# A graph layer in one program: the opening reordered, and the sums of the edge features spread one at a step

## The chip, the cores and the metric

The program runs on one core of a Trainium2 chip. Five engines work side by side, each through its own list of instructions: TensorE (PE: matrix products, with its weight loads, PEld, as a lane of their own in the profile), VectorE (DVE), ScalarE (ACT), GpSimd (POOL) and SyncE (SP). SP issues the ordinary transfers, POOL the indirect ones, which fetch rows by a list of row numbers. The metric is device microseconds of one execution.

## The reference

The layer has 6250 nodes, 206250 edges and 64 features, all in 32-bit floats. The edges are given in the order of their destination `dst`; every node has one edge to itself, and the others are random.

```python
h   = maximum(layernorm(x), 0)                   # 6250 x 64
msg = h[src] + edge_attr                         # 206250 x 64
agg = segment_sum(msg, dst, 6250)                # 6250 x 64
out = x + relu(agg @ W1 + b1) @ W2 + b2          # W1 64 x 128, W2 128 x 64
```

So two sums are wanted for each node: that of `h[src]` over its edges, and that of the edge features over its edges. Which edges belong to a node is known only when the program runs.

## The kernel before

**Sum of h[src] by counts.** For most of the edges the kernel gathers nothing. For each tile of three nodes it counts how often each source occurs among the tile's edges, and multiplies the counts with h, which stays in SBUF as `h2`, 49 blocks of 128 rows. A tile holds up to 127 edges. Three nodes with more edges than that are an "overfull triple"; there is room for 14 of them (`NX`), and each gets a second tile, which starts at its 128th edge.

84 tiles are a **block** of 252 nodes; 23 blocks cover the nodes that are counted. A block is worked in 14 **steps** of 6 tiles. The program is one list of 318 steps written by hand, and all engines get their instructions in that order; so a step number below is a place in the list, not a time. What a step does, in order: first the functions listed for it in the dictionary `before` (and those of `tops`). Then, on odd steps, `count` (line 936): 12 matmuls of a tile each (L943) into one of two PSUM buffers `pc`, and ACT's copy of the counts into `ring` (L952). On every third step DVE makes the rows for 18 more tiles (`rows_of_tiles`, two instructions of L930), on every sixth it encodes the keys of 36 tiles (L913, L919). Then, at the steps 1, 3, 5 and 7 of a block, come 12 or 13 of the 49 `products` of the block before (L962: counts by h, into the PSUM tile `pv`); at step 8 DVE adds `pv` to the sums (L997). So each block has a *product half*, steps 1 to 7, and a *sum half* behind it. Then the MLP of a finished block, where its steps begin (`LAYERS`: at step 11 or 5; the hidden layer L1040, two steps later its product L1048, then an addition and a store). Then what is listed in `later` and `turns` for the step, then the check whether a group of gathered edges may be summed, and last the gathers, as many as are due.

**Sum of the edge features.** 42 nodes in a row are a **chunk**; its edges lie within 1536 rows that follow one another, which SP loads as one tile `feat` (384 KB, six buffers). Of chunks there are six in a block, taken in three pairs. For a pair DVE makes a selector (`chunk_hot`, L487: which edge belongs to which node), at the steps `HOT_AT`; for each chunk PE does 24 pairs of a weight load and a matmul (`chunk_sum`, L498) into a PSUM tile `bank`, at the steps `CHUNKS`, and behind them the load of the chunk three pairs on is issued. At a step of the next block DVE copies the six sums out of PSUM (`take_sums`, L506, at `TAKE`), and PE adds them to that block's `pv` (`chunk_place`, L528, at `PLACE`).

**The gathered edges.** The last 20 groups of 1024 edges are done the other way: POOL gathers their rows of h from a table in DRAM and adds them to the edge features in SBUF (L348, `pfeat`, eight gathers of 128 rows for a group, three buffers). Such a group is summed by 8 matmuls of 128 rows (L559) two steps after its check. The check stands at the steps `GROUPS` of a block. It goes by a clock that the program keeps as it is written (`HEAD_US` 1.7 us for a step of the first block, `STEP_US` 1.04 for each later one, `GATHER_US` 2.0 for a gather): a group is taken at the first such step for which the clock of two steps on is four microseconds past its last gather. Taking a group frees its buffer, and the gathers of the group three further on are queued. POOL has other indirect DMAs in the same queue: the rows of edge data for a set of tiles (`words`, 15 in all), the lists of destinations (`dst`).

**The opening.** Before the steps begin, the layernorm is computed in three parts (`norm_mean` to `norm_h`), the positions of the edges are sought (`fetch_row`, `seek`, `place`), the first two tiles of the chunks' starts are worked out (`chunk_starts`, `chunk_rows`, `chunk_quarters`, `chunk_columns` with its index copy L421, `chunk_index`), and h is written to the table. In the first 14 steps, the first block, there are no products; at the steps `SECOND` seven functions find the overfull triples: ends, flags, ranks, picks, words (60 matmuls of one row or 14, 30 of them in L849), found (L855), fetch. `split_upper` and `split_lower` (L623) turn h into the two forms that the products need; they stand at the steps 10, 15 and 17 and one behind each. `clear` empties the sums at five steps from 18 on.

Of the kernel before, what the change touches and what calls it, by code (L numbers as in the profile page):

```python
# [10 lines left out]
F32 = mybir.dt.float32  # L11
# [11 lines left out]
P = 128  # L23
# [58 lines left out]
SECOND = (9, 10, 11, 12, 13, 14, 15)  # L82
FIRST = 12
PART = (0, 0, 12, 12, 24, 24, 36, 36, HI)
CHUNKS = ((9, 9), (11, 11), (13, 13))
FEATS = 6
FIRST_CHUNKS = ((9, 9), (11, 11), (13, 13))
LAST_CHUNKS = ((5, 5), (9, 9))
HOT_AT = (3, 6, 10)
TAKE = (4, 0)  # L90
PLACE = (6, 3)

GROUPS = (1, 3)
LAST_GROUPS = (1, 5)
LAYERS = {11: 2, 5: 2}
# [54 lines left out]
def gnn_kernel(ctx: ExitStack, tc: tile.TileContext, x, src_t, dst_t, dst_g, edge, w1, b1, w2, b2, out):  # L150
# [677 lines left out]
    def second_picks():  # L828
        flag, ends, prk = flags["flag"], flags["ends"], flags.pop("rank")
        fl = small.tile([P, 4, IC], F32, name="fl")  # L830
        rank, one = fl[:, 0, :], fl[:, 1, :]
        of = fl[:, 2:4, :].rearrange("p a i -> p i a")
        nc.vector.tensor_scalar(of[:, :, 0], nfirst, float(V), None, op0=OP.add)
        nc.vector.tensor_scalar(of[:, :, 1], ends[:, :IC], float(SLOTS), float(EA), op0=OP.add, op1=OP.min)
        nc.vector.tensor_scalar(one, nfirst, float(DUMP), None, op0=OP.subtract)
# [4 lines left out]
        flags["pick"], flags["of"], flags["one"] = pick, of, one  # L840

    def second_words():
        pick, of, one = flags["pick"], flags["of"], flags["one"]
        pxn = ps.tile([P, 2 + NX], F32, tag="po", name="pxn", bufs=1)
        px, pn = pxn[:, :2], pxn[:, 2:]
        for i in range(IC):
            nc.tensor.matmul(px[:NX, :], pick[:, i, :], of[:, i, :], start=(i == 0), stop=(i == IC - 1))
        for i in range(IC):
            nc.tensor.matmul(pn[:1, :], one[:, i:i + 1], pick[:, i, :], start=(i == 0), stop=(i == IC - 1))  # L849
        flags["found"] = px, pn  # L850

    def second_found():
        px, pn = flags.pop("found")
# [3 lines left out]
        nc.vector.tensor_scalar(second_n, pn[:1, :], float(DUMP), float(DUMP), op0=OP.add, op1=OP.min)  # L857
        flags["i"] = second_i
# [64 lines left out]
    def rows_of_tiles(j):  # L923
        if j * HT >= TILES:
            return
# [208 lines left out]
    chunk_quarters(0, 2)  # L1134
    chunk_columns(0, 2, "pc", 2)
# [11 lines left out]
    for g in range(GA + 2, GA + ROWS):  # L1147
# [7 lines left out]
        6: [lambda: chunk_turn(0)],  # L1155
        8: [lambda: place(7, 8)],
# [4 lines left out]
        93: [lambda: chunk_columns(2, NT)],  # L1161
        95: [lambda: chunk_index(2, NT)],
# [12 lines left out]
    for n, f in zip(SECOND, (second_ends, second_flags, second_ranks, second_picks, second_words, second_found, second_fetch)):  # L1175
# [58 lines left out]
    later = {}  # L1234

# [7 lines left out]
    for b in range(NW):  # L1243
        n = b * STEPS
        for u, at_c, at_h in zip(of_block[b], FIRST_CHUNKS if b == 0 else CHUNKS if b < NW - 1 else LAST_CHUNKS, HOT_AT):
            at_step(n + (at_c[0] - 2 if b == 0 else at_h), chunk_hot, u)
            for c in range(units[u][2]):
                at_step(n + at_c[c], chunk_sum, u, c)
        if b < NW - 1:
            at_step(n + STEPS + TAKE[b > 0], take_sums, b)  # L1250
# [206 lines left out]
```

## Time and profile before

| | |
|---|---|
| median of 3 runs | 430.98 us (428.21 to 432.04) |
| the profiled execution | 428.6 us, with a span of 426.6 us |
| instructions in it | 17243 |
| granted clock of PE, mean | 0.978 of full speed |
| busy: PE / PEld | 354.8 / 316.7 us |
| busy: ACT / DVE / POOL | 329.1 / 313.8 / 311.2 us |
| gathers of the groups (L348, pfeat) | 156 of 1693 ns |
| chunk sums (L498) | 3240 pairs |
| counts (L943) | 1904 matmuls |
| products (L962) | 1127 matmuls of 288 ns |

The span is the time from the first instruction to the last in the profiled execution; the time of the same execution is 2.0 us longer. A row of groups reads: line, engine, operation, what is written from what, number, then busy time, mean time of one in ns, and the idle time of the engine ahead of them with what ended most of it. A row of the timeline reads: start, duration, engine, line, operation, tiles and shapes, how many instructions, and in brackets the idle time just before and its end. A busy engine is not one at its peak, since matmuls are pipelined and their ends are modelled.

### The profile page before, as it was taken

Reading aid. Unit: us, or ns where it says so; the run is one execution under the profiler, and the core shown is the slowest. Engines: PE = TensorE matmul, PEld = TensorE weight load, DVE = VectorE, ACT = ScalarE, POOL = GpSimd, SP = SyncE. Lnnn points to the kernel's source line nnn. Section 1 sums busy time; section 2 is a strip of 40 time slices with the busy share of each in tenths; the row PEclk is TensorE's granted clock in tenths of the full one; section 3 lists DMA queues with packets and bytes.
Section 4 is the critical chain, followed back from the end, with each engine's and each line's share of the span. In section 5 each row is a group of like instructions: output and inputs, shape, how many; then the busy total and the mean of one; then the engine's idle time right before and its main releaser. Section 6 shows DMA issues by size and latency. Waiting matters only on the chain.

```text
span 426.6 us, 17243 instructions
## 1 busy us (share of the span) xinstructions
PE 354.8 (83%) x7299; PEld 316.7 (74%) x7300; DVE 313.8 (74%) x813; ACT 329.1 (77%) x378; POOL 311.2 (73%) x230
## 2 busy tenths in 40 slices
PE   2032399989988989969899799999999899999993
PEld 1022378879977878849799698788889789888893
DVE  6677879988996769728698378967697668868531
ACT  5475569898998678957899679887888789888630
POOL 8575588888888888888870868888888748888600
PEclk9999999999999999988999799999999999999997
DMA  7836994969795766939578569669759757977500
GB/s 166 245 112 198 342 225 90 253 144 242 195 241 134 191 155 155 283 48 269 126 177 252 158 136 265 168 160 242 188 133 273 197 156 200 250 179 173 138 15 18
DMA packets 114817, 77.73 MB, mean 182 GB/s; under 512 B 34356, under 2 KB 110252, under 8 KB 114734
## 3 DMA queue, kind: packets, MB, share of 16 engines
q1 hardware_dynamic: 88480, 66.72, 51.6%
q0 software_dynamic: 24016, 9.06, 16.9%
q8 instruction: 59, 0.97, 0.9%
q10 hardware_dynamic: 2238, 0.79, 0.8%
q14 instruction: 24, 0.20, 0.1%
HBM read 72.29 MB, written 4.26 MB: 179 GB/s over the span
## 4 chain that ended last, share of the span: by engine, by line
PE 66%; DVE 10%; ACT 8%; issue 6%; DVEq 0%; ACTq 0%
PE pv L962 25%; PE bank L498 15%; PE pc L943 11%; ACT ring L952 6%; PE ph L1040 3%; PE po L1048 3%; DVE hotb L930 2%; PE bank L559 2%; PE pv L528 2%; PE pk L749 1%; DVE hotf L487 1%; DVE at L913 1%; PE pw L756 1%; DVE xl L607 1%; PE pcols L416 1%
## 5 line engine op out<-in xcount | busy, mean ns | idle before, releaser
L348 POOL DMA_INDIRECT pfeat<-table,src_p x156 | 264.1, 1693 | 72.7 <-issue 42.4
L952 ACT ACTIVATE ring<-pc 128x1764 fp32r<-128x1764 uint8 (+3 forms) x181 | 260.3, 1468 | 45.1 <-PE pc L943 31.5
L962 PE MATMUL pv<-ring,h 128*128 128x252 f32 (+1 forms) x1127 | 156.2, 288 | 0.1
L962 PEld LDWEIGHTS pv<-ring,h 128*128 128x128 f32 x1127 | 138.9, 190 | 0.6 <-issue 0.3
L930 DVE TENSOR_TENSOR hotb<-at,of 127x576 int32<-127x576 bf16 x212 | 118.3, 601 | 1.9 <-DVE of L919 0.5
L498 PE MATMUL bank<-feat,hotf 128*18 128x64 f32 x3240 | 80.3, 229 | 17.1 <-issue 15.9
L943 PE MATMUL pc<-hotb 128*128 128x49 fp8e5 x1904 | 80.7, 187 | 9.5 <-DVE hotb L930 5.9
L943 PEld LDWEIGHTS <-hotb 128*128 128x128 fp8e5 x1904 | 69.2, 99 | 20.3 <-issue 6.1
L498 PEld LDWEIGHTS bank<-feat,hotf 128*18 128x18 f32 x3240 | 57.4, 101 | 30.0 <-issue 26.3
L487 DVE TENSOR_TENSOR hotf<-rel,iota 128x432 f32<-128x432 bf16 x68 | 40.7, 599 | 12.6 <-PE pc L943 10.0
L997 DVE TENSOR_TENSOR sums<-sums,pv 128x252 f32<-128x252 f32 (+3 forms) x28 | 8.4, 327 | 27.7 <-PE pv L962 20.8
L506 DVE COPY after<-bank 128x384 f32<-128x384 f32 (+2 forms) x23 | 12.6, 547 | 21.6 <-PE bank L498 19.2
L913 DVE TENSOR_TENSOR at<-iota_a,kq 128x576 bf16<-128x576 bf16 (+1 forms) x53 | 23.9, 451 | 0.3
L348 POOL DMA_INDIRECT words<-packed,first_i x15 | 17.1, 1140 | 7.4 <-issue 4.0
L1042 ACT ACTIVATE after<-ph,b1s 128x252 f32<-128x252 f32 (+3 forms) x26 | 12.0, 460 | 12.6 <-PE ph L1040 11.7
L348 POOL DMA_INDIRECT sums<-in_dst_g,row_i x15 | 16.7, 1116 | 4.6 <-issue 4.0
L769 ACT ACTIVATE kq<-pk 128x512 bf16<-128x512 f32 (+17 forms) x48 | 17.7, 442 | 3.0 <-PE pc L943 1.0
L1040 PE MATMUL ph<-sums,w1s 128*128 128x252 f32 (+3 forms) x52 | 18.0, 430 | 1.7 <-DVE sums L1009 1.3
L300 PE MATMUL psrc<-shift,src 128*64 128x128 f32 (+1 forms) x16 | 3.9, 419 | 18.2 <-ACT src L297 18.2
L919 DVE TENSOR_TENSOR of<-of,kv 128x288 bf16<-128x288 bf16 (+1 forms) x53 | 16.5, 312 | 2.9 <-ACT sums L366 0.5
L1048 PE MATMUL po<-w2s,after 128*126 128x64 f32 (+3 forms) x104 | 16.9, 287 | 0.8 <-ACT after L1042 0.6
L300 PEld LDWEIGHTS psrc<-shift,src 128*64 128x64 f32 (+1 forms) x16 | 2.8, 188 | 18.2 <-ACT src L297 13.5
(186 smaller groups left out, 318.4 us busy)
## 6 DMA issues: line engine op xcount, KB each, us to landing
feat<-in_edge SPq DMA_DIRECT2D x135, 384.0 KB
pfeat<-in_edge SPq DMA_DIRECT2D x19, 256.0 KB
pfeat<-table,src_p POOLq DMA_INDIRECT x156
out_y<-after SPq DMA_DIRECT2D x23, 63.0 KB
xl<-in_x SPq DMA_DIRECT2D x2, 512.0 KB
table<-xl SPq DMA_DIRECT2D x2, 512.0 KB
after<-in_x SPq DMA_DIRECT2D x4, 252.0 KB
table<-xl SPq DMA_DIRECT2D x1, 544.0 KB
```

What stands on the lines that cost most here:

```text
L348: nc.gpsimd.indirect_dma_start(out=rows, out_offset=None, in_=source, in_offset=bass.IndirectOffsetOnAxis(ap=index, axis=0), compute_op=op)
L487: nc.vector.tensor_tensor(hot_of[u][:, :n].rearrange("p c j w -> p (c j) w"), rel[:, c:c + n].rearrange("p c q k -> p (c q k)").unsqueeze( ...
L498: nc.tensor.matmul(bank[q * QP:q * QP + WQ, at:at + D], hot_of[u][:, c, j, :], feats[u][c][:, j, :], start=(k == 0), stop=(k == JP - 1))
L769: nc.scalar.activation(kq[:, q, at:at + n].rearrange("s i k o -> s (i k) o"), pk[:, q, a:a + n].rearrange("s i k -> s (i k)").unsqueeze(2) ...
L913: nc.vector.tensor_tensor(to[:, :n].rearrange("s i k (m o) -> s (i k) m o", o=2), iota_k.rearrange("s (m o) -> s m o", o=2).unsqueeze(1).t ...
L919: nc.vector.tensor_tensor(pairs_of, pairs_of, kv[:, c:c + n].rearrange("s i k o -> s (i k) o").unsqueeze(2) .to_broadcast([P, 2 * n, WE // ...
L930: nc.vector.tensor_tensor(hot[:SLOTS, :n, c:c + m * A8].rearrange("s i (w a) -> s i w a", a=A8), at[:SLOTS, o:o + n, k].unsqueeze(2).to_br ...
L943: nc.tensor.matmul(pc[:, j * WPC:j * WPC + HI], hot[:, :P], hot[:, P:P + HI], start=True, stop=True)
L952: nc.scalar.activation(to[:, h:z], of[:, h:z, u:v, :V], AF.Copy)
L962: nc.tensor.matmul(pvs[b], h2[:, h, :], ring[:, h, c:c + columns_of_block(b)], start=(h == 0), stop=(h == HI - 1))
L1040: nc.tensor.matmul(ph[:, :n], w1s, agg[:, start[b]:start[b + 1]], start=True, stop=True)
L1048: nc.tensor.matmul(po[:pairs[b], k, :], hid[:, k:2 * pairs[b]:2], w2s, start=True, stop=True)
```

## The change

*Opening.* The second set of rows (`rows_of_tiles(1)`) is made between `chunk_quarters` and `chunk_columns`, ahead of the end of the norm; in its old place, step 0, it is left out. `place(7, 8)` moves from step 8 to 6. The search for the overfull triples has nine functions at the steps 7, 8, 9, 10, 11, 13, 14, 20 and 22 in place of seven at 9 to 15: the node number of a triple becomes a third column of the matmuls that find its tile, so that 30 matmuls of `second_words` go, and is turned into a row later, by one matmul at step 20 (`second_turn`) and a DVE instruction at 22. The third chunk pair of the first block moves from step 13 to 15, which is the second step of block 1 and there stands behind the products; its selector moves to step 13.

*Steady blocks.* Block 1 keeps two chunks at each of the steps 9, 11 and 13. In the blocks 2 to 21 the six chunks stand at 7 and 9, 9 and 11, 13 and 15 (the last is step 1 of the next block). Those at 7 and 15 are put ahead of the products of their step (the new dictionary `soon`); of the two at 9 the one that comes first in its pair goes into `turns`, behind the other. `take_sums` and `chunk_place` go from steps 0 and 3 of the next block to 2 and 5 for these blocks, since the sixth sum now ends at step 1. The second pair's selector is made at step 5 in place of 6.

*Groups and MLP.* The checks for a group stand at the steps 1 and 7 of a block in place of 1 and 3, the second MLP at 7 in place of 5. Two steps in the work on later chunk starts come one and two steps sooner.

```diff
-SECOND = (9, 10, 11, 12, 13, 14, 15)
+SECOND = (7, 8, 9, 10, 11, 13, 14, 20, 22)
...
-CHUNKS = ((9, 9), (11, 11), (13, 13))
+EARLY_CHUNKS = ((9, 9), (11, 11), (13, 13))
+CHUNKS = ((7, 9), (9, 11), (13, 15))
 FEATS = 6
-FIRST_CHUNKS = ((9, 9), (11, 11), (13, 13))
+FIRST_CHUNKS = ((9, 9), (11, 11), (15, 15))
 LAST_CHUNKS = ((5, 5), (9, 9))
-HOT_AT = (3, 6, 10)
-TAKE = (4, 0)
-PLACE = (6, 3)
-
-GROUPS = (1, 3)
+HOT_AT = (3, 5, 10)
+TAKE = (4, 0, 2)
+PLACE = (6, 3, 5)
+
+GROUPS = (1, 7)
 LAST_GROUPS = (1, 5)
-LAYERS = {11: 2, 5: 2}
+LAYERS = {11: 2, 7: 2}
...
     def second_words():
...
         for i in range(IC):
             nc.tensor.matmul(px[:NX, :], pick[:, i, :], of[:, i, :], start=(i == 0), stop=(i == IC - 1))
-        for i in range(IC):
-            nc.tensor.matmul(pn[:1, :], one[:, i:i + 1], pick[:, i, :], start=(i == 0), stop=(i == IC - 1))
-        flags["found"] = px, pn
+        flags["found"] = px
...
+    def second_turn():
+        pn = ps.tile([P, NX], F32, tag="po", name="psecond", bufs=1)
+        nc.tensor.matmul(pn[:1, :], flags.pop("nodes"), ident[:NX, :NX], start=True, stop=True)
+        flags["turned"] = pn
+
+    def second_nodes():
+        nc.vector.tensor_scalar(second_n, flags.pop("turned")[:1, :], float(DUMP), float(DUMP), op0=OP.add, op1=OP.min)
...
     def rows_of_tiles(j):
-        if j * HT >= TILES:
+        if j * HT >= TILES or j in hots:
             return
...
     chunk_quarters(0, 2)
+    rows_of_tiles(1)
     chunk_columns(0, 2, "pc", 2)
...
         5: [lambda: chunk_nodes(0)],
-        6: [lambda: chunk_turn(0)],
-        8: [lambda: place(7, 8)],
+        6: [lambda: chunk_turn(0), lambda: place(7, 8)],
...
-        93: [lambda: chunk_columns(2, NT)],
-        95: [lambda: chunk_index(2, NT)],
+        92: [lambda: chunk_columns(2, NT)],
+        93: [lambda: chunk_index(2, NT)],
...
             at_step(n + (at_c[0] - 2 if b == 0 else at_h), chunk_hot, u)
             for c in range(units[u][2]):
-                at_step(n + at_c[c], chunk_sum, u, c)
+                k = at_c[c]
+                when = later
+                if 1 < b < NW - 1:
+                    when = soon if k in (7, STEPS + 1) else turns if (k, c) == (9, 0) else later
+                when.setdefault(n + k, []).append(lambda u=u, c=c: chunk_sum(u, c))
         if b < NW - 1:
-            at_step(n + STEPS + TAKE[b > 0], take_sums, b)
+            at_step(n + STEPS + TAKE[min(b, 2)], take_sums, b)
             for u in of_block[b]:
-                at_step(n + STEPS + PLACE[b > 0], chunk_place, u)
+                at_step(n + STEPS + PLACE[min(b, 2)], chunk_place, u)
...
             encode(n // (EB // ST) + 1)
+        for f in soon.pop(n, []):
+            f()
         if b and 1 <= s < FRESH:
             products(b - 1, PART[s], PART[s + 1])
```

25 lines of the change are left out of this document (13 added, 12 removed).

## The prediction

> **What bounds the kernel now.** I read the page first, for the chain and the groups.
>
> ```profile
> span 426.6 us, 17243 instructions
> ...
> PE 66%; DVE 10%; ACT 8%; issue 6%; DVEq 0%; ACTq 0%
> ...
> L348 POOL DMA_INDIRECT pfeat<-table,src_p x156 | 264.1, 1693 | 72.7 <-issue 42.4
> L952 ACT ACTIVATE ring<-pc 128x1764 fp32r<-128x1764 uint8 (+3 forms) x181 | 260.3, 1468 | 45.1 <-PE pc L943 31.5
> ```
>
> TensorE (PE) holds 66% of the chain that ended last, but ScalarE (ACT) copies counts for 260.3 us and GpSimd (POOL) gathers for 264.1 us, so each half of a block has to be looked at by itself. The busy times by window give this (length, then busy time of PE, its weight loads (PEld), VectorE (DVE), ACT and POOL, the granted clock, DMA). The first is block 1, the second all of the blocks 2 to 21, the next three are single blocks (from one start of products to the next), the last two the product half and the sum half of an ordinary one.
>
> ```profile
> 63.66:78.74 15.08, 13.88 (x298) 12.53 (x295) 13.87 (x37) 14.21 (x12) 12.89 (x8) 1.00 0.54 120
> 78.74:397.01 318.27, 295.23 (x6294) 264.34 (x6289) 244.68 (x630) 267.32 (x289) 250.01 (x155) 0.98 0.75 192
> 139.33:158.63 19.30, 17.44 (x352) 15.34 (x349) 13.14 (x39) 12.39 (x12) 16.25 (x11) 1.00 0.65 159
> 174.43:196.87 22.44, 18.77 (x331) 15.79 (x327) 11.59 (x28) 15.30 (x18) 18.70 (x13) 0.85 0.62 153
> 227.12:246.22 19.10, 16.96 (x321) 14.63 (x317) 10.87 (x27) 14.15 (x16) 9.25 (x7) 0.84 0.65 186
> 353.33:361.70 8.37, 8.37 (x128) 8.07 (x124) 7.91 (x27) 7.95 (x12) 7.15 (x5) 1.00 0.82 205
> 361.70:367.83 6.13, 5.90 (x203) 4.96 (x200) 4.89 (x12) 5.44 (x6) 5.21 (x4) 1.00 0.76 203
> ```
>
> The 20 steady blocks take 318.27 us. Without the three long ones (60.84) the other 17 take 15.14 each: a product half of 8.4, in which PE is busy throughout, and so 6.7 for the sum half. In the sum half quoted PE has holes (4.96 of 6.13 loading weights) and ACT needs 5.44: ACT is the floor there, 0.7 below. The waits of the steady stretch say what the holes are.
>
> ```profile
> PEld bank L498 <- issue: 24.4, 52, 0.6
> ACT ring L952 <- PE pc L943: 19.7, 39, 2.5
> POOL pfeat L348 <- DMA pfeat<-in_edge: 19.5, 2, 13.0
> ```
>
> Fifty-two times PE stops in the middle of a feature sum with no semaphore to wait for, 24.4 us or 1.2 per block. The timeline shows when.
>
> ```profile
> 316.27 0.47 PE L943 MATMUL pc<-hotb 128*128 128x49 fp8e5 x12
> ...
> 316.68 0.84 PE L498 MATMUL bank<-feat,hotf 128*18 128x64 f32 x37
> 316.71 1.69 POOL L348 DMA_INDIRECT pfeat<-table,src_p  x1 [0.30 <-issue]
> ...
> 317.97 0.23 PEld L498 LDWEIGHTS bank<-feat,hotf 128*18 128x18 f32 x10 [0.61 <-issue]
> ```
>
> A gather starts at 316.71, PE issues 37 pairs of the sum, stops, and goes on 1.26 us after the start of the gather. I read it so: for about 1.2 us of each gather PE gets no new instructions and lives on those it holds, some 32 to 37 pairs. Products, 49 of them in the 8.37 us of a half, never use these up; a run of 48 sums does in 0.8 us.
>
> Two blocks hit this hard: two short gathers in a row leave PE starved.
>
> ```profile
> 237.00 0.99 POOL L348 DMA_INDIRECT words<-packed,first_i  x1 [0.30 <-issue]
> ...
> 238.29 1.42 POOL L348 DMA_INDIRECT words<-packed,first_i  x1 [0.30 <-issue]
> 238.31 0.15 PEld L498 LDWEIGHTS bank<-feat,hotf 128*18 128x18 f32 x4 [0.59 <-issue]
> ...
> 239.06 0.15 PEld L498 LDWEIGHTS bank<-feat,hotf 128*18 128x18 f32 x4 [0.59 <-issue]
> ```
>
> Four pairs run per 0.75 us, and the clock granted in these two blocks is 0.85 and 0.84. Over 15.14 they cost 7.30 and 3.96, of which the clock is 0.15 x 22.44 = 3.4 and 0.16 x 19.10 = 3.1.
>
> **The change, part by part.** The sum starts from the profiled execution, 428.6 us with a span of 426.6; the median of the runs is 430.98, 2.4 above it.
>
> *The head.* Rows of its timeline:
>
> ```profile
> 38.16 0.16 DVE L421 CAST cols_i<-pcols 128x2 int32<-128x2 f32 x1 [1.59 <-PE pcols L416]
> ...
> 44.18 1.12 DVE L930 TENSOR_TENSOR hotb<-at,of 127x576 int32<-127x576 bf16 x2
> ...
> 45.35 0.41 PE L943 MATMUL pc<-hotb 128*128 128x49 fp8e5 x6 [5.51 <-DVE hotb L930]
> ...
> 50.49 0.61 DVE L487 TENSOR_TENSOR hotf<-rel,iota 128x432 f32<-128x432 bf16 x1 [0.95 <-ACT rel L447]
> ...
> 59.59 0.91 PE L849 MATMUL pxn<-pick,fl 128*1 128x14 f32 x30
> ...
> 61.12 0.15 DVE L855 CAST second_i<-pxn 14x1 int32<-14x1 f32 x1 [2.83 <-PE pxn L849]
> ...
> 61.26 1.96 PE L498 MATMUL bank<-feat,hotf 128*18 128x64 f32 x48
> ...
> 63.66 2.67 PE L962 MATMUL pv<-ring,h 128*128 128x252 f32 x11
> ...
> 63.90 1.22 DVE L623 TENSOR_TENSOR h<-xl,sums 128x1024 fp32r<-128x1024 f32 x1
> ```
>
> Rows 1 (1.12 on DVE) move from behind the norm into the hole of 1.59 before the index copy: nothing in front of the norm gets later, all of DVE behind it comes 1.12 sooner, and the 5.51 for which PE waited goes. That is no gain of 5.51: the second quarter of the first products needs L623, which ends at 65.1 on DVE. DVE's holes on the way there are 0.95 and 2.83. The second hole is the wait for the overfull triples: the 30 matmuls of L849 go (0.91; two come back at step 20, under the clears), and the rest is asked for earlier. Against it: the first step of the triples now stands at step 7, so the count of step 7, and the copies by ACT behind it, wait on PE's queue for DVE's placement, two rows and ends. Bounds: 0 (the new wait eats all) and 1.12 + 0.95 + 2.83 = 4.9. I take 2.5, the middle: one hole shrinks by half. The third pair (1.96) leaves the front of the first products for step 15. In block 1, which gets it, PE has a cover of 15.08 - 13.88 = 1.2 us. A clean run of 48 costs 0.80 there (row below), so I add 0; 0.8 if the cover is gone.
>
> *One chunk at a step, blocks 2 to 21.* Three runs of 48 (steps 9, 11, 13) become 24 at 7 and 15, before the products, 24 + 24 at 9, and 24 at 11 and 13. What a run costs:
>
> ```profile
> 309.38 0.50 PE L943 MATMUL pc<-hotb 128*128 128x49 fp8e5 x12
> ...
> 309.72 1.65 PE L962 MATMUL pv<-ring,h 128*128 128x252 f32 x12
> ...
> 404.03 0.87 PE L498 MATMUL bank<-feat,hotf 128*18 128x64 f32 x48
> 404.83 0.47 PE L943 MATMUL pc<-hotb 128*128 128x49 fp8e5 x12
> ```
>
> 48 pairs take 0.80 with the switch behind them, so 24 take 0.40. The switch from counts into a sum costs 0.41 - 0.34 = 0.07 (316.27 to 316.68 against 309.38 to 309.72). From a sum into products no row shows: between 0 and the 0.16 that are left in 0.80 if a pair costs 0.0135. I take 0.07 + 0.08. The product half grows by 2 x 0.55 = 1.1, to 9.5. The Trainium skill (TensorE: Matmul & The Clock Gate, Wait — 56ns, not 53.3ns?) speaks against this: matmuls never start closer than about 25 ns, which makes 0.60 of 24 pairs, a product half of 9.9 and of the whole sum about 429. The quoted run is at 17 ns a pair with its switch, so the measurement decides. The sum half loses 48 pairs (0.8) and some of its stops. 24 pairs in front of products hardly use up what PE holds, the 48 of step 9 do, 12 counts and 24 sums (36 pairs) just do; I take 0.5 of 1.2 left, 0.7 gone. 6.7 - 0.8 - 0.7 = 5.2, below ACT's 5.44, so ACT sets it: 5.5. The block is 15.0 against 15.14: -0.14, 17 times, -2.4. Bounds: the switch (0 to 0.24 each) and the stops (0.2 to 1.0 left, partly under ACT) give 14.8 to 15.7.
>
> The loads behind each sum on the queue of SyncE (SP) move with it; each has a block of some 15 us until its use. Sums taken at step 2 and placed at 5 in place of 0 and 3: DVE waits there for PE anyway, and 8 is where the products are added. The hidden layer at 7 in place of 5: its two products then stand among the sums. Groups at 1 or 7 in place of 1 or 3: followed by the program's own clock, seven of eighteen come eight steps sooner and one four later, which frees gather buffers earlier. The 19.5 us that POOL waited are not on the path:
>
> ```profile
> 400.38 2.60 POOL L348 DMA_INDIRECT pfeat<-table,src_p  x1 [0.30 <-DVE odd_i L899]
> ...
> 411.37 0.43 PE L559 MATMUL bank<-after,pfeat 128*64 128x42 f32 x8
> ```
>
> The last gather has 8.4 us to spare. Chunk indices two steps sooner: 0.
>
> *The starved blocks.* Whether short gathers meet a run is phase, and all phases move. I take off the clock's part of one, 3.4; bounds 0 and 11.3, and a new one would cost as much.
>
> Sum: 428.6 - 2.5 - 2.4 - 3.4 = 420.3, and 2.4 for the median: 422.7.
>
> **Rivals.** *No change, 430:* both starved blocks recur and the stops only move, since each gather still holds PE for 1.2 us. Steady 0 to +0.2 a block, 0 to 3.4 in 17, head -2.5: 426.1 to 429.5, 428.5 to 432 by the median. For it: 155 gathers in 20 blocks, as before. Against it: a third of the pairs go to where they cannot stop PE. The Trainium skill (TensorE: Matmul & The Clock Gate, Part 1) gives PE's queue 64 entries, 32 pairs, and by it every place with counts and 24 sums still stops; the 37 pairs issued at 316.68 leave just room for 36.
>
> *Slower, 438:* the sum half is ACT's. Moving 48 pairs from where PE has holes to where it has none pays twice: the product half becomes 9.7 (switches at 0.24 with some wait), the sum half stays at 6.0, since the hidden layer's product at 13 now waits for ACT behind two copies (0.5). 15.7 - 15.14 = 0.56, 17 times 9.5; with the head -2.5: 435.6, 438.0. It decides as soon as the sum half stays above 5.64 beside a product half of 9.5. For it: PE busy for 8.37 of 8.37 in the product half, with no hole that could take 24 pairs. Against it: stops of 1.2 a block that ACT would then cover.
>
> *Larger gain, 409:* both starved blocks go (11.3), and with the stops all gone and ACT's copies running into the next block, 0.5 a block, 8.5: 428.6 - 2.5 - 8.5 - 11.3 = 406.3, 408.7. POOL allows it: its gathers end at 403.0 - 19.5 = 383.5 if they do not wait, 8 behind a loop of which 27 are taken off.
>
> **How the numbers follow.** Forecast 0.40, larger gain 0.10, no change 0.28, slower 0.22. About 1% (4.3 us) is what a measurement of this kernel can tell from no change. Faster by more: 0.50; within: 0.28; slower: 0.22. The forecast's own range is 415 to 427. The range 410 to 438 leaves out half of the larger gain and half of the slower case, 0.16.
>
> **What would show it.** Rows 1: the 5.51 on PE gone, the index copy still near 38.2. Triples: the 2.83 on DVE halved, products at about 61. Steady: the line PEld bank L498 from issue below 12 us; the product half near 9.5 and the sum half near 5.5; ACT's waits for PE shift to the product half. I am wrong if the sum half stays above 6 (then ACT or new PE waits hold it), if stops keep 24 us, or if windows at a clock of 0.85 grow in number.

## The result, and the profile after

The changed kernel takes 442.19 us (median of 4 runs, 437.04 to 447.82) where the kernel before takes 429.6 beside it: a ratio of 1.0277, with an interval of 1.0219 to 1.0334. (Two of these four executions were in a slower state, which the kernel before shows at times too; medians are over all executions, ratios, here and below, over those of the faster state alone, so a ratio need not be the quotient of two medians.) It is slower by 12 us; the forecast was 422.7 with a range of 410 to 438. Its profiled execution takes 439.97 us with a span of 438.2. From the page, the chain by engine and three groups (columns as before), and then two of these groups as they were before the change:

```profile
span 438.2 us, 17199 instructions
...
PE 67%; DVE 11%; ACT 11%; issue 8%; another core or an unknown queue 1%; ACTq 0%; DVEq 0%
...
L959 ACT ACTIVATE ring<-pc 128x1764 fp32r<-128x1764 uint8 (+3 forms) x181 | 260.3, 1473 | 61.9 <-PE pc L950 43.1
...
L499 PE MATMUL bank<-feat,hotf 128*18 128x64 f32 x3240 | 79.3, 228 | 13.7 <-ACT after L562 7.3
...
L1055 PE MATMUL po<-w2s,after 128*126 128x64 f32 (+3 forms) x104 | 17.4, 291 | 9.0 <-ACT after L1049 7.2
```

```profile
L498 PE MATMUL bank<-feat,hotf 128*18 128x64 f32 x3240 | 80.3, 229 | 17.1 <-issue 15.9
...
L1048 PE MATMUL po<-w2s,after 128*126 128x64 f32 (+3 forms) x104 | 16.9, 287 | 0.8 <-ACT after L1042 0.6
```

ACT copies the same counts in the same 260.3 us, but is idle in front of them for 61.9 where it was 45.1, most of it waiting for PE; and PE waits for ACT, at lines where it hardly did before. Neither is busy throughout: each waits for the other in turn. The busy times by window (columns as in the prediction): block 1, the steady blocks, and of an ordinary block the stretch from its first product to its last, and the stretch from there to the next block's first product.

```profile
59.92:77.98 18.06, 16.15 (x360) 14.57 (x360) 15.23 (x42) 15.50 (x14) 15.32 (x10) 1.00 0.67 162
77.98:408.66 330.68, 302.29 (x6277) 266.74 (x6272) 240.24 (x626) 266.84 (x288) 250.93 (x156) 0.97 0.74 184
314.07:322.69 8.62, 8.62 (x137) 8.17 (x132) 7.74 (x24) 7.64 (x10) 6.92 (x5) 1.00 0.67 161
322.69:329.79 7.10, 6.03 (x196) 4.95 (x192) 6.06 (x17) 5.60 (x7) 0.42 (x1) 1.00 0.87 241
```

The steady blocks take 330.68 where they took 318.27: these 12.4 are the whole loss. Ahead of them 0.8 is won (77.98 for 78.74; the first products begin 3.7 sooner, but block 1 takes 18.06 for 15.08), behind them nothing changes (438.2 - 408.66 = 29.5; before, 426.6 - 397.01 = 29.6). The last window takes 7.10. Of its six sums only the one of step 7 has left it: the one of step 15, which the prediction books with the product half, stands at its end, ahead of the next products.

To compare the halves as the prediction cuts them, I took them from the starts of the matmuls, with the sum of step 15 in the product half. On average over the 20 blocks the product half takes 9.56 us where it took 8.56, and the sum half 6.95 where it took 7.35. The waits of the steady blocks:

```profile
ACT ring L959 <- PE pc L950: 35.9, 47, 3.6
...
PEld po L1055 <- ACT after L1049: 9.1, 14, 1.4
...
PEld bank L499 <- issue: 7.7, 15, 0.6
PEld bank L499 <- ACT after L562: 7.2, 7, 1.6
```

The stops without a semaphore fell from 24.4 us to 7.7, as forecast (below 12). In their place stand two waits for ACT: of the MLP's product for the hidden layer (L1049), and of a sum for ACT's copy of a group (L562). The timeline of the block above shows both, PE first and then ACT:

```profile
322.94 0.53 PE L499 MATMUL bank<-feat,hotf 128*18 128x64 f32 x24
323.62 0.67 PE L560 MATMUL bank<-after,pfeat 128*64 128x42 f32 x16 [0.15 <-DVE after L550]
324.89 0.53 PE L499 MATMUL bank<-feat,hotf 128*18 128x64 f32 x24 [0.60 <-ACT after L562]
...
326.22 0.69 PE L1047 MATMUL ph<-sums,w1s 128*128 128x252 f32 x2
326.75 0.46 PE L950 MATMUL pc<-hotb 128*128 128x49 fp8e5 x12
327.14 0.53 PE L499 MATMUL bank<-feat,hotf 128*18 128x64 f32 x24
327.98 0.68 PE L1055 MATMUL po<-w2s,after 128*126 128x64 f32 x4 [0.31 <-ACT after L1049]
```

```profile
323.10 1.64 ACT L959 ACTIVATE ring<-pc 128x1764 fp32r<-128x1764 uint8 x1 [0.90 <-PE pc L950]
324.64 0.20 ACT L562 ACTIVATE after<-bank 128x42 f32<-128x42 f32 x1
325.93 1.64 ACT L959 ACTIVATE ring<-pc 128x1764 fp32r<-128x1764 uint8 x1 [1.08 <-PE pc L950]
327.47 0.47 ACT L1049 ACTIVATE after<-ph,b1s 128x252 f32<-128x252 f32 x1
```

ACT works in order. The group is ready at 324.3, its copy of 0.20 stands behind a copy of counts of 1.64 and starts at 324.64, and the next sum, which writes to the same PSUM tile, waits for it. The hidden layer's copy starts at 327.47 for the same reason; between the hidden layer and its product PE now has 12 counts and 24 sums, where it had 12 counts and 48 sums. The same place in a block before the change, where ACT stood idle when the hidden layer came and PE did not wait for its product:

```profile
320.32 0.69 PE L1040 MATMUL ph<-sums,w1s 128*128 128x252 f32 x2
...
320.85 0.46 PE L943 MATMUL pc<-hotb 128*128 128x49 fp8e5 x12
...
321.11 0.47 ACT L1042 ACTIVATE after<-ph,b1s 128x252 f32<-128x252 f32 x1 [0.60 <-PE ph L1040]
...
321.24 1.25 PE L498 MATMUL bank<-feat,hotf 128*18 128x64 f32 x48
...
322.42 0.68 PE L1048 MATMUL po<-w2s,after 128*126 128x64 f32 x4
```

For a full account I took the start of each matmul in the trace and added up the time to the next one's start, by the kinds of the two, from block 1's first product to block 21's. The last two columns belong to an experiment below (both kernels with the gathers of the groups left out).

| from one matmul to the next | before | after | before, no gathers | after, no gathers |
|---|---|---|---|---|
| sum to sum | 72.8 | 50.7 | 39.3 | 37.7 |
| sum to MLP product | 3.0 | 12.8 | 5.5 | 12.5 |
| group to sum | 0 | 8.0 | 0 | 6.8 |
| sum to products | 0 | 6.3 | 0 | 5.8 |
| counts to sum | 6.9 | 11.5 | 7.3 | 11.7 |
| counts to products | 2.0 | 1.6 | 2.1 | 1.1 |
| to and from groups and placing, but to sums and from products to placing | 5.3 | 9.0 | 5.3 | 7.7 |
| all others | 228.2 | 230.7 | 222.4 | 221.0 |
| all | 318.3 | 330.7 | 281.9 | 304.3 |

22.1 us were saved inside the sums; 34.5 came in beside them.

### The profile page after: what moved, and what is told of

Same layout as the page of the kernel before. It is cut to its first block, busy times and chain, and to the rows that moved or that the text cites. A ratio compares the mean times of both kernels' runs of the same rounds, so it can differ in the third digit from the quotient of the medians.

```text
span 438.2 us, 17199 instructions
## 1 busy us (share of the span) xinstructions
PE 361.6 (83%) x7271; PEld 318.8 (73%) x7272; DVE 310.7 (71%) x814; ACT 328.3 (75%) x378; POOL 305.7 (70%) x230
## 4 chain that ended last, share of the span: by engine, by line
PE 67%; DVE 11%; ACT 11%; issue 8%; another core or an unknown queue 1%; ACTq 0%; DVEq 0%
PE pv L969 28%; PE bank L499 12%; PE pc L950 11%; ACT ring L959 5%; PE po L1055 4%; DVE hotb L937 3%; PE bank L560 3%; PE ph L1047 2%; PE pv L529 2%; ACT after L1049 2%; PE pk L750 1%; ACT sums L367 1%; DVE hotf L488 1%; DVE at L920 1%
## 5 line engine op out<-in xcount | busy, mean ns | idle before, releaser
L349 POOL DMA_INDIRECT pfeat<-table,src_p x156 | 259.8, 1665 | 82.7 <-issue 42.7
L959 ACT ACTIVATE ring<-pc 128x1764 fp32r<-128x1764 uint8 (+3 forms) x181 | 260.3, 1473 | 61.9 <-PE pc L950 43.1
L499 PE MATMUL bank<-feat,hotf 128*18 128x64 f32 x3240 | 79.3, 228 | 13.7 <-ACT after L562 7.3
L950 PE MATMUL pc<-hotb 128*128 128x49 fp8e5 x1904 | 79.4, 188 | 2.2 <-issue 1.3
L499 PEld LDWEIGHTS bank<-feat,hotf 128*18 128x18 f32 x3240 | 54.1, 101 | 23.1 <-issue 9.2
L1004 DVE TENSOR_TENSOR sums<-sums,pv 128x252 f32<-128x252 f32 (+3 forms) x28 | 8.4, 327 | 40.7 <-PE pv L969 34.5
L1061 DVE TENSOR_TENSOR after<-po,after 126x128 f32<-126x128 f32 (+3 forms) x26 | 7.5, 290 | 26.6 <-PE po L1055 24.2
L1055 PEld LDWEIGHTS po<-w2s,after 128*126 128x126 f32 (+3 forms) x104 | 13.9, 193 | 12.9 <-ACT after L1049 9.9
L1049 ACT ACTIVATE after<-ph,b1s 128x252 f32<-128x252 f32 (+3 forms) x26 | 11.9, 458 | 13.1 <-PE ph L1047 11.1
L349 POOL DMA_INDIRECT sums<-in_dst_g,row_i x15 | 15.6, 1037 | 4.6 <-issue 3.7
```

Source lines behind the costliest of these rows:

```text
L349: nc.gpsimd.indirect_dma_start(out=rows, out_offset=None, in_=source, in_offset=bass.IndirectOffsetOnAxis(ap=index, axis=0), compute_op=op)
L499: nc.tensor.matmul(bank[q * QP:q * QP + WQ, at:at + D], hot_of[u][:, c, j, :], feats[u][c][:, j, :], start=(k == 0), stop=(k == JP - 1))
L950: nc.tensor.matmul(pc[:, j * WPC:j * WPC + HI], hot[:, :P], hot[:, P:P + HI], start=True, stop=True)
L959: nc.scalar.activation(to[:, h:z], of[:, h:z, u:v, :V], AF.Copy)
L1049: nc.scalar.activation(outs[b][:, :n], ph[:, :n], AF.Relu, bias=b1s)
L1055: nc.tensor.matmul(po[:pairs[b], k, :], hid[:, k:2 * pairs[b]:2], w2s, start=True, stop=True)
```

## The experiments

**What the times are compared with.** Kernels that ran one after the other on the same chip are called a session. The kernel before took 429.6, 423.8 and 424.5 us in three of the sessions and 405.0 to 405.4 in three others, so each kernel is compared with the runs of the kernel before beside it. The traces say what differs: in the first kind PE stops in the sums, in the second it doesn't. One chip showed both, 423.8 in one session and 405.1 in a later one. Below, "with stops" and "without stops" mean these sessions.

### One part at a time (with stops)

The opening alone: `SECOND`, `FIRST_CHUNKS`, `rows_of_tiles(1)` and `place(7, 8)` as in the change, all else as before.

> The kernel before with the opening of the changed kernel alone: rows 1 sooner, the overfull triples in nine functions, the third chunk pair of block 0 at step 15. In the changed kernel the first products begin at 59.92 in place of 63.66, and block 1's products (77.98 for 78.74) give most of it back: 1.42 for the 48 sums that now stand in the first product half, and about 1.5 for a group of gathered edges (0.60, and 0.95 of waiting for ACT's copy of it) that the opening alone doesn't put there. Theory 'the opening is worth 2.3 by itself and the loss is all in the steady blocks': block 1's products begin 2.3 us sooner, 427.3 us. Rival 'the opening only borrows': the 3.7 are lost again in block 0's product half whatever the group does, block 1's products begin within 0.8 of 78.7 and the time is 429 to 430.

Measured: 418.57, ratio 0.9908 (0.9867 to 0.995). Products begin at 58.57 and block 1's at 74.49; the kernels of the second and third run below, which have the opening of before and ran beside it, reach block 1's at 77.01 and 77.60. So the opening alone is worth 2.5 to 3.1 at block 1, and in the time about 4 of 423.8. The rival, that it only borrows, falls.

The chunks alone:

```diff
-CHUNKS = ((9, 9), (11, 11), (13, 13))
+EARLY_CHUNKS = ((9, 9), (11, 11), (13, 13))
+CHUNKS = ((7, 9), (9, 11), (13, 15))
-HOT_AT = (3, 6, 10)
+HOT_AT = (3, 5, 10)
-TAKE = (4, 0)
-PLACE = (6, 3)
+TAKE = (4, 0, 2)
+PLACE = (6, 3, 5)
```

> The kernel before with the chunks of the blocks 2 to 21 at one a step, their sums taken and placed two steps later and the chunk indices sooner; the opening, the steps for groups (1, 3) and for the MLP (11, 5) stay as before. Theory A, PE waits for ACT's copies, which ACT makes in order: in the changed kernel's 20 blocks the time inside the sums falls by 22.1 us (72.8 to 50.7); against that stand some 13 for the switches, 9.8 in front of the MLP's products and 8.0 to 10 behind groups that stand in front of a sum. Without the new places of the groups the last goes: 429.6 - 22 + 13 + 10 = 430.6 (428 to 433). Theory B, the product half pays more than the sum half can give back, whatever the groups do: the blocks cost 0.6 more each, 441 to 442.

Measured: 436.05, ratio 1.0341 (1.0239 to 1.0443). Theory A's sum fell: the chunks by themselves lose as much as the whole change. Against the trace of the opening alone (same session, steady blocks as before) the 20 blocks take 326.5 for 314.5. Inside the sums only 8.4 were saved (68.0 to 59.6), and 5.2 inside the counts; the time in front of the MLP's products grew from 3.5 to 14.4, switches into and out of sums by 9.4 (sum to products 5.8, counts to sum 6.8 to 11.9, counts to products 2.6 to 1.2), and groups that no longer stand beside the placing cost some 3. Theory B had the size, and its account of the halves holds: the product half grew from 8.52 to 10.08 and the sum half fell only from 7.21 to 6.22. What it didn't name is the largest item, the wait in front of the MLP's product.

The groups alone:

```diff
-GROUPS = (1, 3)
+GROUPS = (1, 7)
```

> The kernel before with the steps for groups at 1 and 7 in place of 1 and 3, nothing else. Here a group at step 7 is summed at step 9 behind a run of 48 sums, and 12 counts stand between it and the next sum. Theory A: the wait for ACT's copy of the group is mostly under those counts, at most 0.5 for each of 7 groups: 430 to 433. Theory C, the earlier groups themselves cost (8 matmuls twice over among the sums, gathers that start elsewhere): 435 or more. Theory B: 430.

Measured: 423.77, ratio 1.0048 (1.0003 to 1.0093). Theory C, 1.3% or more, falls; theory A and theory B's 430 are too near each other to be told apart. Counts to sum grew from 6.8 to 11.8, and the weight loads of sums wait 5.2 us for ACT's copy of a group: that copy is not quite under 12 counts.

The group behind both sums of step 9 (in the changed kernel):

```diff
-    when = soon if k in (7, STEPS + 1) else turns if (k, c) == (9, 0) else later
+    when = soon if k in (7, STEPS + 1) else later
```

> The changed kernel with the two sums of step 9 one behind the other, and so the group, where there is one, behind both and not between them. Theory A: the waits of sums for ACT's copy of the group (7 times, 8.0 us in the intervals from the group to the sum) go, and 48 sums in a row stop a little more often: 434 to 437 beside 442.2 (440.0 in the profiled run). Theory B: the group's place doesn't matter, 440 to 442.

Measured: 429.08 where 423.82 is before, ratio 1.0183 (1.0078 to 1.0287). The 8.0 from a group to a sum are gone in its trace; 3.1 come back from counts to sum (14.6 for 11.5), since ACT's copy now meets the next sum. The changed kernel itself did not run beside it, and its ratio elsewhere lies between 1.015 and 1.028, so the gain in the time can't be told and theory B isn't excluded by it.

### Which sums were cover (without stops)

Only the first pair apart, and only the third:

```diff
-CHUNKS = ((9, 9), (11, 11), (13, 13))
+CHUNKS = ((7, 9), (11, 11), (13, 13))      # first pair apart
+CHUNKS = ((9, 9), (11, 11), (13, 15))      # third pair apart (TAKE 2, PLACE 5)
```

> The kernel before, but in the blocks 2 to 21 only the first pair of chunks is taken apart: a chunk at step 7, ahead of the products, and one at 9, then two at 11 and two at 13 as before (sums taken at 0 and placed at 3; chunk indices sooner). One sum more stands in each product half, and the MLP's product at step 13 keeps its 48 sums for cover. From the trace of the kernel with all the chunks spread and no other change: a sum in front of products costs 0.149 behind it and some 0.11 ahead, less the 0.025 that the change from counts to products cost. Theory A (what spreading costs is, first, a switch of 0.24 for each of the two sums in a product half, and second 0.64 for each of 17 MLP products at step 13, which lose half of their cover): 20 x 0.24 = 4.8 more, and 4 to 8 fewer in the stops of the sums: -0.8% to +0.3%. Theory B (any sum in the product half delays ACT, the MLP's wait is only where that shows): half of the loss of all the chunks spread, +1.5% or more.

> The kernel before, but in the blocks 2 to 21 only the third pair of chunks is taken apart: two at 9, two at 11, one at 13 and one at step 1 of the next block, ahead of the products (sums taken at 2 and placed at 5; chunk indices sooner). As with the first pair apart there is one sum more in each product half; here the MLP's product at step 13 stands behind 24 sums and not 48. Theory A: 4.8 for the switches, 17 x 0.64 = 10.9 for the MLP's product, 4 to 8 fewer in the stops: +1.8% to +2.8%, and 2 to 3 per cent over the kernel with the first pair apart. Theory B: the same as that kernel, within 1%.

Measured: 398.88, ratio 0.9872 (0.9834 to 0.991), and 403.57, ratio 0.9986 (0.9955 to 1.0017). Both are faster than forecast, for a reason that the last two sections of experiments show: where PE doesn't stop, the end of the kernel before waits for gathers. The blocks themselves got longer, 292.4 and 295.8 where the kernel before, in another session without stops, has 284.8. The third pair apart is 1.1% behind the first, in theory A's direction and half its size; of the 4.6 us between the spans of the two, 1.5 lie ahead of block 1 and 3.5 in the blocks. In front of the MLP's products stand 11.1 against 8.7. So keeping the 48 sums at step 13 saves some of that wait, but not most: it is 5.3 in the kernel before, without stops. The other item is the placing at step 5, which parts it from the groups: placing to counts 2.1 for 0.7, products to group 3.1 for 0.2, placing to group 0.3 for 1.6, together some 3.

The changed kernel with the group behind both sums and the product of the MLP at step 15:

```diff
-LAYERS = {11: 2, 7: 2}
+LAYERS = {11: 4, 7: 2}
```

> The changed kernel with the two sums of step 9 one behind the other (as run before, ratio 1.018), and the product of the MLP that begins at step 11 two steps later, at step 15 behind the products there. Theory A: PE's time in front of these products, 11.5 us in the trace without the delay for 21 of them, falls to about 0.15 each, and with it 6 to 8 us of the time: ratio 1.000 to 1.005. Theory B (ACT sets the sum half in any case): PE waits for ACT elsewhere, ratio 1.015 to 1.02.

Measured: 403.96, ratio 0.997 (0.9946 to 0.9994), a little below theory A's range. The changed kernel itself has 1.0152 in another session without stops (below), so the two waits for ACT are worth about 1.8%, some 7 us; the blocks take 298.0 for 306.8. Time in front of the MLP's products fell from 12.4 to 3.5, 1.6 of it for the four that are left behind sums, but the 10 value turns of step 15, which use the same PSUM buffer, now wait for DVE to have read the product (the time in front of value turns grew from 1.8 to 7.2, and PE waits 3.8 there for DVE): part of a wait removed comes back as the next user's.

### With and without the gathers

First on two chips, by themselves, and the two kernels again for a trace:

```diff
-            queue.append((GATHER_US, lambda j=j: gather(
-                parts_of[g][:, j, :], table[:, :], src_p[:, (g - GA) * J + j:(g - GA) * J + j + 1], OP.add)))
+            queue.append((GATHER_US, lambda: None))
```

> The kernel before without the 156 gathers of the last 20 groups on POOL (their share of the sum is left out; the feature rows of these groups are still loaded and summed, and the list of instructions is otherwise the same). If the stops of PE in the middle of the sums come from the gathers, the time inside the sums of the 20 blocks falls from 68 to 73 us to about 46 to 48 (2796 intervals of 0.017), the stops from 'issue' on the sums go to under 5 us, no block is starved, and the time falls by 20 to 25 us, to about 0.945. If the stops are PE's own and only happen to stand beside gathers (code loading on its own schedule), the stops stay at 20 us and the time falls by less than 2%.

> The kernel before, unchanged, for a trace from the same chip as the kernels beside it. Two chips have shown two pictures of the sums: on the first and second, PE stops in them for 15 to 25 us of the 20 blocks; on the third, where the first pair apart ran, there is no stop at all (2776 intervals inside the sums take 38.4 us). If the stops belong to the chip, this kernel and the changed one beside it show either both stops or both none; if they belong to the program, this one shows them on any chip, with 65 to 75 us inside the sums.

> The changed kernel, unchanged, beside the one before. Theory A: the change saves only stops and pays switches (39 x 0.24), the waits of the MLP's products and of sums behind a group. Where the chip shows no stops there is nothing to save, and the loss is larger than the 2.8% of the first chip: 4 to 5%. Where it shows them, 2 to 3.5%. Theory B (the loss is not tied to the stops): 2.8% on any chip.

> The changed kernel without the 156 gathers of the last groups (their share of the sum is left out, all else stands). The kernel before without them took 0.962 of itself with them, and no stop was left in it. Theory A: without gathers there are no stops to save, and only the costs of the change are left, 10 us of switches, 5 to 11 in front of the MLP's products, up to 8 behind the groups, less 3 to 4 of the opening: its 20 blocks take 15 to 22 us more than the 281.4 of the kernel before without gathers. Theory B (the change costs because of the gathers): within 6 us of 281.4.

Measured: the kernel before without gathers 388.88 in a session without stops, ratio 0.9618 (0.9555 to 0.968), 39.3 inside the sums. In one with stops: the kernel before again 425.16, 70.3 inside the sums; the changed one 431.7, ratio 1.0183 (1.01 to 1.0266, where theory A has 2 to 3.5%), 51.4 inside; and without gathers 418.83, ratio 0.988 (0.9799 to 0.9961), 41.9 inside. There, the stops on the sums fall from 23 (9.7 us) to 5 (3.4) when the gathers go: they come with the gathers, but, as the next four show, not with the gathers alone. Nor are the gathers all that differs between the sessions: the changed kernel's blocks without them take 312.0 here, 30.6 above the 281.4 of the kernel before without them in the other session, where theory A expected 15 to 22.

Then all four on one chip, in a session without stops:

> The kernel before, unchanged, for a trace from the same chip as the three beside it. If the stops of PE in the sums come from the gathers: 63 to 73 us inside the sums of the 20 blocks on a chip that shows them, 38 to 40 on one that doesn't.

> The changed kernel, unchanged. Theory A: 1.8 to 2.8% slower where the chip shows the stops, 3 to 5% where it doesn't.

> The kernel before without the 156 gathers of the last groups (their share of the sum is left out, all else stands), on the same chip as the other three. Theory A (stops and starving come from the gathers): inside the sums 38 to 42 us, the 20 blocks 281 to 286; where the chip shows stops, 25 us or more less than with the gathers. Rival (the 281.4 seen before belonged to the chip): 300 us or more.

> The changed kernel without the 156 gathers (their share of the sum is left out). Theory A: without stops to save only the costs are left; 18 to 30 us over the kernel before without gathers on the same chip, against 8 to 13 between the two with gathers on a chip that shows stops. Theory B (the price of the change depends on the gathers): no more than with gathers.

Measured: 404.59 for the trace of the kernel before (405.41 the runs beside); 411.29, ratio 1.0152 (1.0107 to 1.0198); without gathers 388.29, 0.9589 (0.9542 to 0.9636), and 408.69, 1.0083 (1.0044 to 1.0121). The 20 blocks by window: before, after, before without gathers, after without gathers.

```profile
75.28:360.07 284.79, 273.78 (x6288) 253.32 (x6287) 243.92 (x632) 262.76 (x289) 240.01 (x148) 1.00 0.83 213
```

```profile
73.00:379.77 306.77, 287.61 (x6277) 258.24 (x6272) 240.20 (x629) 264.40 (x288) 253.06 (x158) 1.00 0.81 200
```

```profile
74.30:356.25 281.95, 273.51 (x6289) 253.10 (x6287) 240.95 (x631) 262.37 (x289) 13.43 (x12) 1.00 0.67 199
```

```profile
72.90:377.15 304.25, 286.72 (x6278) 257.74 (x6273) 237.69 (x628) 264.02 (x288) 13.88 (x12) 1.00 0.64 186
```

The change costs its blocks 22.0 us with gathers and 22.3 without: 1.1 a block. That is its bare price, and the table above says what it is made of: 7.0 in front of the MLP's products (12.5 - 5.5), 6.8 behind the groups, 9.1 for switches (5.8 + 4.4 - 1.1 of counts to products), 2.4 around groups and placing, less 1.6 inside the sums and 1.4 elsewhere. Where PE stops, the change takes part of the stops away and the 22 shrink to 12.4 (first session) and 8.3 (322.5 for 314.2, when both ran again). Theory A's answer holds: only stops are saved, and the costs stand by themselves. In these four the stops are missing with the gathers running; the one row that the kernel before has of them is

```profile
PEld bank L498 <- issue: 0.4, 1, 0.4
```

Why then is the changed kernel only 1.5% behind, where theory A has 3 to 5%, when its blocks lose 22? It is 2.3 sooner at block 1, and the kernel before has 402.7 - 360.07 = 42.6 us behind its blocks, the changed one 409.9 - 379.77 = 30.1. Without the gathers the kernel before has 385.9 - 356.25 = 29.7, so it is the gathers that hold it. The end of the kernel before, in windows:

```profile
360.07:371.40 11.33, 10.81 (x230) 10.01 (x226) 5.57 (x23) 8.07 (x7) 9.50 (x7) 1.00 0.53 108
371.40:381.30 9.90, 4.74 (x48) 3.73 (x46) 2.01 (x6) 0.68 (x2) 6.63 (x5) 0.76 0.22 25
381.30:388.60 7.30, 7.30 (x32) 6.97 (x31) 0.49 (x2) 1.15 (x3) 0.00 (x0) 0.50 0.03 9
388.60:396.60 8.00, 7.04 (x31) 6.08 (x30) 0.90 (x3) 0.73 (x2) 0.00 (x0) 0.50 0.04 11
```

PE comes to its last block at 371.4, before the gathers are through (the last ends at 379.2). It is busy for half of the next 10 us, in which it waits 4.3 us for the gathers' data, and then runs at a granted clock of 0.50 to the end. With the blocks at their quickest the gathers are the bound, and the wait for them costs twice: its own length and the clock.

### The opening and the first pair apart together

> The opening of the changed kernel with the first pair of chunks apart (7 and 9; 11 and 11; 13 and 13) and the groups and the MLP where they were before. The two parts alone gave 0.991 and 0.987; if they add up, 0.975 to 0.982. If the gain of the first pair apart was that chip's, 0.985 to 0.995.

> The opening of the changed kernel alone, a second time, now beside the kernel with the first pair of chunks apart. If the opening is worth 2.3 to 4 us on any chip: 0.990 to 0.994 where the chip shows PE's stops. On a chip without stops the time of the kernel before is set at the end by the gathers (its last blocks end 12.6 us later after the steady blocks than those of the changed kernel), and a sooner opening gains at most what the gathers begin sooner: 0.995 to 1.000.

> The opening of the changed kernel and the first pair of chunks apart, a second time. On a chip with stops: the switches of the 20 sums (20 x 0.24 = 4.8) against 4 to 8 us of stops, so within 0.7% of the opening alone. On one without: the 4.8 are paid in blocks that end before the gathers do, and the two are again within 0.7% of each other.

Measured: the two together 419.75, ratio 0.9898 (0.9846 to 0.9951), with stops, so the gains don't add up there. In a session without: the opening alone 406.42, ratio 1.0027 (1.0003 to 1.0051); with the first pair apart 397.29, ratio 0.9793 (0.9761 to 0.9825). The opening alone gains nothing there, as expected: its blocks end at 358.96 in place of 360.07 (another session) and 42.4 follow. That the first pair apart would be within 0.7% of it was wrong. Its blocks are slower and end at 366.64, but 30.2 follow: it meets the gathers (last end 376.4) without waiting, and the clock row of its page has no 5 at the end. The same explains the 0.9872 of the first pair apart alone (29.6 behind its blocks). Of the kernels that leave nothing out this one is the fastest without stops; with stops it can't be told from the opening alone (0.9908).

## Why the prediction was wrong

**The step that failed** is "6.7 - 0.8 - 0.7 = 5.2, below ACT's 5.44, so ACT sets it: 5.5". It took ACT's busy time as the floor of the sum half, as if PE and ACT worked side by side. They work in a ring: PE makes the hidden layer, ACT must first end a copy of counts (1.64) and then make its own (0.47), and PE's next product waits. The sums between the hidden layer and its product were cover for that, and I priced the leaving of 48 sums at their length alone, "-0.8". The wait grew by 9.8 us in the steady blocks of the first trace (3.0 to 12.8) and by 7.0 without gathers. The sum half was to lose 1.2 (6.7 to 5.5) and lost 0.4 (7.35 to 6.95), though the stops fell by more than forecast; without stops it grew, from 5.68 to 5.97. How the wait divides between the sums taken from step 13 and the ones taken ahead of the hidden layer isn't settled: with the first pair alone apart, and all 48 left at step 13, it is 8.7 against 5.3.

**The groups.** "The 19.5 us that POOL waited are not on the path" was true and beside the point: the gathers are off the path, but the matmuls of a group (16 in the trace, 8 in the program) and ACT's copy of them are not. At step 7 they come to step 9, between two sums that write to the same PSUM tile. I followed the gathers' clock and not the instructions that move; 8.0 us for 7 groups, and 3.7 around groups and placing that no longer stand side by side.

**The switch** was mis-sized: 0.15 a run, with 0.24 as its bound; without gathers it is 0.149 behind the sums, 0.113 ahead, less the 0.025 that counts to products cost, 0.24; 39 runs cost 9.1 to 10.6 us in the three kernels for which the table or the text above gives them. The product half grew by 1.0 where 1.1 was forecast; as the switch cost more, and 7 groups left it for step 9, that agreement is in part luck. On the rule of the Trainium skill (TensorE: Matmul & The Clock Gate, Wait — 56ns, not 53.3ns?) the traces don't agree: from the first of 24 sums at 320.45 to the first product at 320.91 are 0.46, 19 ns a pair, the switch included. These matmuls write in turn to four parts of `bank` of 32 partitions each, and no run here tries others of that size.

**The stops** went as argued. Counted as more than 0.2 us from one matmul of a run to the next, there were 53 in 59 runs of 48 before (40 runs had one or more), and 13 in 99 runs of 24 after (11 runs), with 4 more in the 10 runs of 48 that are left. I took 0.7 a block, 14 in all; 22.1 were saved inside the sums. The estimate that the prediction worked out from the 64 entries that the Trainium skill (TensorE: Matmul & The Clock Gate, Part 1) gives PE's queue, that places with 12 counts and 24 sums would still stop, came true for few of them. But the stops are no property of the kernel alone: in three sessions they were absent, and in the one of these where the changed kernel ran it loses 22 in its blocks with next to nothing to set against it.

**The starved blocks** stayed: I took one off (3.4). Four blocks of the changed kernel have a clock of 0.84 to 0.92, where two had 0.84 and 0.85 before.

**The opening** was right by itself: 2.5 forecast, 2.5 to 3.1 measured at block 1. The index copy stays at 38.21, the wait of 5.51 is gone, products begin at 59.92. In the changed kernel 0.8 is left in this trace; in the two later sessions with a trace of both it begins block 1's products 4.1 and 2.3 sooner (75.20 for 79.33, 73.00 for 75.28). The third pair, at 0 for me and 0.8 at most, costs 1.4 there, because PE is slow in that place:

```profile
59.92 2.92 PE L969 MATMUL pv<-ring,h 128*128 128x252 f32 x12 [0.91 <-ACT ring L959]
62.77 1.48 PE L499 MATMUL bank<-feat,hotf 128*18 128x64 f32 x48
64.19 0.68 PE L950 MATMUL pc<-hotb 128*128 128x49 fp8e5 x12
64.70 1.65 PE L969 MATMUL pv<-ring,h 128*128 128x252 f32 x12
...
71.01 0.86 PE L499 MATMUL bank<-feat,hotf 128*18 128x64 f32 x48
71.80 0.67 PE L560 MATMUL bank<-after,pfeat 128*64 128x42 f32 x16
72.40 0.47 PE L950 MATMUL pc<-hotb 128*128 128x49 fp8e5 x12
73.82 0.80 PE L499 MATMUL bank<-feat,hotf 128*18 128x64 f32 x36 [0.95 <-ACT after L562]
```

48 sums take 1.48 here and 0.86 eight microseconds later. And the first group, now in block 1, takes 0.60 and the wait of 0.95 for ACT's copy of it.

**The rival** "slower, 438" had the price of the switch (0.24) and the place of the wait ("the hidden layer's product at 13 now waits for ACT behind two copies", 0.5), and gave 435.6 for a profiled run of 439.97. The wait is well sized: 9.8 us over 21 products are 0.47 each. Its first clause, that ACT sets the sum half, was not the reason: ACT waited more than before. And that its sum comes near is in part luck, since it leaves out the 22.1 saved inside the sums and the 8.0 behind the groups. It stood at 0.22. The rows to rank it higher were there: a copy of counts of 1.47 and one of the hidden layer of 0.46 in front of a product that would keep 12 counts and 24 sums, 0.9, for cover. The larger gain's "POOL allows it" was misread too: its own sum takes 22.3 off the loop, not 27, and where the blocks did become that quick, gathers that end behind them held the last block (42.6 us behind the blocks for 29.7 without gathers).

## What to carry to other kernels

Work that stands between an operation and the answer of another engine is cover: before moving it, or work ahead of it, add up what the other engine, in order, has to do first, and compare that with what is left between. When a step moves, price every instruction that comes with it and what it will stand between; operations of one kind next to each other save a tenth of a microsecond or two at each border. And when quicker blocks only arrive sooner at a transfer's end, look at the time behind the last block as well as at the blocks.

## What the runs showed of the hardware

The stops of PE under gathers come and go between sessions, on one and the same chip: with the same instructions and the same 156 gathers the kernel before spends 70 to 73 us inside the sums of 20 blocks in one kind of session and 39.0 in the other, and its time is 424 to 430 or 405. In a session with stops, leaving the gathers out brought the time inside the changed kernel's sums from 51.4 to 41.9. What decides between the two kinds stays open.

PE starts slowly though the granted clock of the windows there is 1.00: 12 counts take 0.68, 12 products 2.92 and 48 sums 1.48 until some 5 us into the first products, then 0.47, 1.65 and 0.86.

After ten microseconds in which PE is busy for half, the granted clock is 0.50, and it stays there for the 21 us that are left, though PE is busy for all of the first 7.3 of them; in the changed kernel of the same session, which comes to its last block later and keeps PE busy, it stays at 1.00 until 10 us from the end.
